# Two layers over neighbour lists on one core: one multiply per list in layer 0; gates ahead of a shared projection and slots added in pairs in layer 1

## The chip, the core and the metric

The kernel runs on one core of a Trainium2 chip. The metric is the device time of one execution in microseconds. The core's engines run side by side, each through its own instructions in order: PE (matrix multiplies; PEld is its weight load), DVE (vector), ACT (scalar), POOL (GpSimd) and SP (used here to issue DMAs). They wait for each other through semaphores. Data moves between the chip's memory (HBM) and the on-chip memories, SBUF (128 partitions) and PSUM (the accumulators of PE), by 16 DMA engines.

## The reference

There are 3327 nodes with 512 features and one sparse symmetric 0/1 adjacency matrix. Layer 0 is an attention layer with four heads of 128, layer 1 a gated sum of an attention part and a plain neighbour sum. Each layer is added to its input and normalised.

```python
# layer 0
feats = jnp.einsum('nf,hfo->hno', X, W)
e_s = jnp.einsum('hno,ho->hn', feats, a_self)
e_n = jnp.einsum('hno,ho->hn', feats, a_neigh)
logits = e_s[:, :, None] + e_n[:, None, :]
logits = jnp.where(logits > 0, logits, LRELU_ALPHA * logits)
logits = logits + NEG_INF * (1.0 - A)[None, :, :]
attn = jax.nn.softmax(logits, axis=-1)
out = jnp.einsum('hnm,hmo->hno', attn, feats)
...
x = _layernorm(x + relu(out + b))
# layer 1 (adj_a and adj_b are the same matrix)
attn_a = sigmoid(concatenate([adj @ x, x]) @ Wa.T + ba)
attn_b = sigmoid(concatenate([adj @ x, x]) @ Wb.T + bb)
h = x @ W_sa
scores = s_left[:, None] + s_right[None, :]
e = jnp.where(adj != 0, jnp.exp(-leaky_relu(scores, 0.01)), 0.0)
attn = e / (jnp.sum(e, axis=1, keepdims=True) + 1e-05)
x_a = attn @ h
x_b = adj @ (x @ W_gcnb) + b_gcnb
x = _layernorm(x + sigmoid(attn_a * x_a + attn_b * x_b))
```

## The kernel before

The kernel doesn't multiply with the adjacency matrix. A first stage reads it once, turns each node's row into a list of neighbour numbers, computes layer 0's features and attention logits for every node, and writes them as rows of 520 numbers into a table in HBM (`table0`). The nodes are sorted by the length of their lists and dealt into 26 tiles of 128, so that the tiles' lists have the fixed lengths in `CAPS`, from 23 slots down to 5, 253 in all. Tile 0 is handled as two lists of 12 and 11 slots, each other tile as one list: 27 lists.

Both layers then go tile by tile, in groups of four (`GRP`). `gather` (line 368) issues one indirect DMA per slot on POOL (line 373): 128 rows of the table, one per partition, into slot s of a buffer `g` of up to 15 slots. There are three such buffers in each layer, so the gather of a list waits until the list three before it has been read by all that use it.

Layer 0 (`attend`, line 403) fetches the tile's x rows (line 406), adds the logits (line 413), takes a softmax over the slots (lines 416 to 428, with the exponential on ACT), and multiplies each slot's 512 features by the attention of its head. That last step is one DVE instruction per slot (line 437), except for each third slot, where ACT does it in four instructions, one per head (line 435). PE sums the slots in PSUM by multiplying them with the identity (line 442); an fp32 matmul goes through PE in two passes. DVE adds bias and x, and takes the statistics. After each group the tiles are normalised (line 470) and `publish` (line 448) writes them as rows of a second table, `table1`, again by an indirect DMA on POOL (line 458). Layer 1's gathers read `table1`, so they start when the last tile has been published.

Layer 1 (`combine`, line 487) gathers a list in the same way, forms the attention weights `e` (lines 492 to 498) and their sum, and the two gates, `gate[:, 0:1]` and `gate[:, 1:2]`, from columns of the gathered rows (lines 503 to 511); `gate[:, 3:4]` is the first gate divided by the sum of e. PE sums all slots unweighted into `acc` (line 518, one PSUM bank). DVE sums them weighted by e into `sw`, one instruction per slot (lines 520 and 522). Both sums are transposed by PE (line 529), copied by ACT (lines 524 and 531), and multiplied by their own weight matrices into two banks, `pa` and `pb` (line 534). Lines 538 to 540 apply the gates to the two products and add them, on ACT and DVE. Then come the sigmoid (as a tanh, line 542), the residual, the statistics, and after each group of four the normalisation (line 552) and the write of the output rows, indirect DMAs on POOL (line 553).

The order of the instructions on each engine is not the order of the source: a scheduler places them by its own estimates. So a publish or an output write stands between gathers on POOL's queue, the logits of one list among another list's DVE work, and parts of one tile's `acc` ahead of the projections of the tile before it on PE. A dense version of the layers follows under a flag, for inputs whose lists don't fit; it does not run here.

Of the kernel before, what the change touches and what calls it, by code (L numbers as in the profile page):

```python
# [8 lines left out]
F32 = mybir.dt.float32  # L9
AF = mybir.ActivationFunctionType  # L10
ALU = mybir.AluOpType
# [3 lines left out]
P = 128  # L15
# [41 lines left out]
def sparse_pass(  # L57
# [28 lines left out]
    nc = tc.nc  # L86
    N, F = out.shape
    NP = x.shape[0]
    H, _, FO = W0.shape
    KT = F // P  # L90
# [11 lines left out]
    ident = const.tile([P, P], F32, name="ident")  # L102
# [5 lines left out]
    bias_g = const.tile([P, F], F32, name="bias_g")  # L108
# [10 lines left out]
    with tc.tile_pool(name="p0", bufs=1) as p0, tc.tile_pool(name="p0s", bufs=2) as p0s:  # L119
# [73 lines left out]
        with tc.tile_pool(name="p0f", bufs=2, space=PSUM) as psf, tc.tile_pool(  # L193
            name="p0c", bufs=1, space=PSUM
        ) as psc, tc.tile_pool(name="p0v", bufs=2, space=PSUM) as psv:
            for c0 in range(0, NP, CH):
# [7 lines left out]
                for g0 in range(0, NT, 4):  # L204
                    g = min(4, NT - g0)
                    a = p0s.tile([P, 4, CH], F32, tag="at", name=f"at{c0}_{g0}", bufs=10)
# [5 lines left out]
                for t in range(t0, t0 + nt):  # L212
                    pf = psf.tile([P, 2, 512], F32, tag="pf", name=f"pf{t}")
                    for k in range(KT):
                        for hh in range(2):
                            nc.tensor.matmul(  # L216
                                pf[:, hh, :HC], xc[:, k, (t - t0) * P : (t - t0 + 1) * P], w0[:, k, hh, :],
                                start=(k == 0), stop=(k == KT - 1),
# [8 lines left out]
                for half, m0, m1 in ((0, 0, 16), (1, 16, NT)):  # L227
                    for m in range(m0, m1):
                        s, c = (m - m0) // 4, (m - m0) % 4
                        nc.tensor.matmul(  # L230
                            pc[32 * c : 32 * c + 32, half, :cw], pow2[:, s, :], at[m // 4][:, m % 4, :cw],
                            start=(s == 0), stop=(m + 4 >= m1),
# [55 lines left out]
        with tc.tile_pool(name="p0r", bufs=1, space=PSUM) as psr:  # L288
# [46 lines left out]
            pb = psr.tile([P, 1], F32, name="pbad")  # L335
# [14 lines left out]
        with nc.allow_non_contiguous_dma(reason="four vectors of 512, onto partitions"):  # L350
            for i, w in enumerate((Wa, Wb)):
                for s in range(2):
                    src = w[0:1, s * F : (s + 1) * F].rearrange("o (k p) -> p (o k)", p=P)
# [48 lines left out]
    with tc.tile_pool(name="m0", bufs=2) as m0, tc.tile_pool(name="m0p", bufs=2, space=PSUM) as ps:  # L402
        def attend(j, mv):
            c = CAPS[j]
            xg = m0.tile([P, F], F32, tag="xg", name=f"xg{j}", bufs=3)
            nc.gpsimd.indirect_dma_start(
                out=xg, out_offset=None, in_=x, in_offset=bass.IndirectOffsetOnAxis(ap=own[:, j, :], axis=0)
            )
            got = gather(m0, table0, j, "g0")
            w = m0.tile([P, S, H], F32, tag="w", name=f"w{j}")  # L410
            lk = m0.tile([P, S, H], F32, tag="lk", name=f"lk{j}")
            for s0, n, g in got:
                nc.vector.tensor_add(  # L413
                    w[:, s0 : s0 + n, :], g[:, :n, F : F + H], es[:, j : j + 1, :].to_broadcast([P, n, H])
                )
            nc.vector.scalar_tensor_tensor(w[:, :c], w[:, :c], 0.2, w[:, :c], ALU.mult, ALU.max)
            mx = m0.tile([P, 1, H], F32, tag="mx", name=f"mx{j}")


            nc.vector.tensor_scalar(lk[:, :c, 0], valid[:, j, :c], 1e30, -1e30, ALU.mult, ALU.add)  # L420
            nc.vector.tensor_add(w[:, :c], w[:, :c], lk[:, :c, 0:1].to_broadcast([P, c, H]))
            nc.vector.tensor_reduce(mx[:, 0, :], w[:, :c].rearrange("p s h -> p h s"), AX.X, ALU.max)
            nc.vector.tensor_sub(w[:, :c], w[:, :c], mx.to_broadcast([P, c, H]))  # L423
            nc.scalar.activation(w[:, :c], w[:, :c], AF.Exp)  # L424
            den = m0.tile([P, 1, H], F32, tag="den", name=f"den{j}")
            nc.vector.tensor_reduce(den[:, 0, :], w[:, :c].rearrange("p s h -> p h s"), AX.X, ALU.add)
            nc.vector.reciprocal(den, den)
            nc.vector.tensor_mul(w[:, :c], w[:, :c], den.to_broadcast([P, c, H]))  # L428
            acc = ps.tile([P, F], F32, tag="acc", name=f"acc{j}")
            for s0, n, g in got:  # L430
                for s in range(s0, s0 + n):
                    gv = g[:, s - s0, 0:F].rearrange("p (h o) -> p h o", h=H)
                    if s % 3 == 2:
                        for h in range(H):
                            nc.scalar.activation(gv[:, h, :], gv[:, h, :], AF.Copy, scale=w[:, s, h : h + 1])  # L435
                    else:
                        nc.vector.tensor_tensor(  # L437
                            gv, gv,
                            w[:, s, :].rearrange("p (h o) -> p h o", o=1).to_broadcast([P, H, FO]),
                            ALU.mult,  # L440
                        )
                    nc.tensor.matmul(acc, ident, g[:, s - s0, 0:F], start=(s == 0), stop=(s == c - 1))  # L442
            y = x1[:, j, 0:F]
            nc.vector.tensor_add(y, acc, bias0)
            nc.vector.scalar_tensor_tensor(y, y, 0.0, xg, ALU.max, ALU.add)
            stats(m0, y, mv)

        def publish(j):
            pt = ps.tile([P, KT, P], F32, tag="pt", name=f"x1t{j}")
            for k in range(KT):  # L450
                nc.tensor.transpose(pt[:, k, :], x1[:, j, k * P : (k + 1) * P], ident)
            xt1 = m0.tile([P, KT, P], F32, tag="xt1", name=f"xt1_{j}")
            nc.scalar.copy(xt1, pt)
            pcol = ps.tile([P, NCOL], F32, tag="pcol", name=f"pcol{j}")
            for k in range(KT):
                nc.tensor.matmul(pcol, xt1[:, k, :], v1[:, k, :], start=(k == 0), stop=(k == KT - 1))
            nc.scalar.copy(x1[:, j, F : F + NCOL], pcol)
            nc.gpsimd.indirect_dma_start(
                out=table1[:, :], out_offset=bass.IndirectOffsetOnAxis(ap=own[:, j, :], axis=0),
                in_=x1[:, j, :], in_offset=None, bounds_check=N - 1, oob_is_err=False,  # L460
            )


        for js in groups:
            mv = m0.tile([P, GRP, 2], F32, tag="mv", name=f"mv0_{js[0]}")
            for i, j in enumerate(js):
                attend(j, mv[:, i, :])
            r = rsqrt(m0, mv, len(js), f"0_{js[0]}")
            for i, j in enumerate(js):
                nc.vector.tensor_scalar(  # L470
                    x1[:, j, 0:F], x1[:, j, 0:F], mv[:, i, 0:1], r[:, i : i + 1], ALU.subtract, ALU.mult
                )
                publish(j)


    with tc.tile_pool(name="w1", bufs=1) as w1, tc.tile_pool(name="m1", bufs=2) as m1, tc.tile_pool(
        name="m1p", bufs=2, space=PSUM
    ) as ps:
        wsa = w1.tile([P, KT, F], F32, name="wsa")
        nc.sync.dma_start(wsa, W_sa.rearrange("(k p) o -> p k o", p=P))  # L480
        wg = w1.tile([P, KT, F], F32, name="wg")
# [5 lines left out]
        def combine(j, mv):  # L487
            c = CAPS[j]
            got = gather(m1, table1, j, "g1")
            e = m1.tile([P, S], F32, tag="e", name=f"e{j}")  # L490
# [6 lines left out]
            gate = m1.tile([P, 6], F32, tag="gate", name=f"gate{j}")  # L497
# [12 lines left out]
            nc.scalar.activation(gate[:, 0:2], gate[:, 0:2], AF.Tanh, scale=0.5)  # L510
            nc.vector.tensor_scalar(gate[:, 0:2], gate[:, 0:2], 0.5, 0.5, ALU.mult, ALU.add)
            nc.vector.tensor_mul(gate[:, 3:4], gate[:, 0:1], gate[:, 2:3])

            acc = ps.tile([P, F], F32, tag="acc", name=f"acc1_{j}", bufs=1)
            sw = m1.tile([P, F], F32, tag="sw", name=f"sw{j}")
            for s0, n, g in got:
                for s in range(s0, s0 + n):
                    nc.tensor.matmul(acc, ident, g[:, s - s0, 0:F], start=(s == 0), stop=(s == c - 1))  # L518
                    if s == 0:
                        nc.vector.tensor_scalar(sw, g[:, 0, 0:F], e[:, 0:1], None, ALU.mult)  # L520
                    else:
                        nc.vector.scalar_tensor_tensor(sw, g[:, s - s0, 0:F], e[:, s : s + 1], sw, ALU.mult, ALU.add)  # L522
            sp = m1.tile([P, F], F32, tag="sp", name=f"sp{j}")
            nc.scalar.copy(sp, acc)  # L524
            outs = []
            for src, wt, tag in ((sw, wsa, "pa"), (sp, wg, "pb")):
                pt = ps.tile([P, KT, P], F32, tag="pt", name=f"pt{tag}{j}")
                for k in range(KT):
                    nc.tensor.transpose(pt[:, k, :], src[:, k * P : (k + 1) * P], ident)  # L529
                sT = m1.tile([P, KT, P], F32, tag="sT", name=f"sT{tag}{j}")  # L530
                nc.scalar.copy(sT, pt)
                po = ps.tile([P, F], F32, tag=tag, name=f"{tag}{j}")
                for k in range(KT):
                    nc.tensor.matmul(po, sT[:, k, :], wt[:, k, :], start=(k == 0), stop=(k == KT - 1))  # L534
                outs.append(po)
            za = m1.tile([P, F], F32, tag="za", name=f"za{j}", bufs=GRP + 2)
            zb = m1.tile([P, F], F32, tag="zb", name=f"zb{j}")
            nc.scalar.activation(za, outs[0], AF.Copy, scale=gate[:, 3:4])
            nc.vector.tensor_add(zb, outs[1], bias_g)
            nc.vector.scalar_tensor_tensor(za, zb, gate[:, 1:2], za, ALU.mult, ALU.add)  # L540

            nc.scalar.activation(za, za, AF.Tanh, scale=0.5)
            nc.vector.scalar_tensor_tensor(za, za, 0.5, x1[:, j, 0:F], ALU.mult, ALU.add)
# [446 lines left out]
```

## Time and profile before

| | us |
|---|---|
| median of 3 runs (lowest, highest) | 1273.58 (1273.38, 1276.06) |
| the profiled execution | 1273.58 |
| its span | 1271.8 |
| lists and table 0, to 206 | 206 |
| lists written to HBM and read back, 206 to 274 | 68 |
| layer 0: first x rows to the first gather of layer 1, 274 to 712 | 438 |
| layer 1: to the last output write, 712 to 1258 | 546 |

The span runs from the first to the last recorded instruction; the time of the execution has 1.8 us more around it. The stages overlap by little, because layer 0 needs all lists and layer 1 all published rows. The profile page gives for the whole span:

```profile
PE 906.7 (71%) x2790; PEld 456.8 (36%) x2790; DVE 693.0 (54%) x2045; ACT 219.4 (17%) x639; POOL 657.6 (52%) x688
```

These shares are means over stages of different kinds, and no engine is near 100%. What a change in a stage is worth must be read within that stage, from what the engines wait for there. A group's line in the profile reads: line of the source, engine, operation, what is written from what, count, then the busy time in us, the mean of one instruction in ns, and the idle time of the engine just ahead of such instructions with what ended most of it. A timeline's line reads: start and length in us, engine, line, operation, count if several equal ones follow each other, and in brackets the idle time before it and what ended it; "issue" is idle time in which the profile shows nothing waited for.

### The profile page before, as it was taken

To read this page: it belongs to the slowest core of one execution; us is meant where nothing else is said; L and a number is where in the kernel's file an instruction comes from. 1 tells how busy PE (TensorE), PEld (TensorE's weight loads), DVE (VectorE), ACT (ScalarE), POOL (GpSimd) and SP (SyncE) were. 2 spreads that over 40 slices of the span, in tenths; PEclk is the share of its full clock that TensorE was granted. 3 is DMA by queue.
4 is the path that set the end of the run, shared out by engine and by line. 5 is a ranking of instruction groups with operands and counts; after the bars stand their busy time and mean duration, and the time that the engine had idled before them with its cause. 6 is when DMAs were issued, how large, how long until landed. Compare 5 with 4: busy or idle time off the path is not lost. (4 is left out here: it accounts for less than half of the span.)

```text
span 1271.8 us, 10106 instructions
## 1 busy us (share of the span) xinstructions
PE 906.7 (71%) x2790; PEld 456.8 (36%) x2790; DVE 693.0 (54%) x2045; ACT 219.4 (17%) x639; POOL 657.6 (52%) x688
## 2 busy tenths in 40 slices
PE   3999941001985869798677475796996969989891
PEld 1756520000433325444234122343443434444440
DVE  4599893002555564557565046755565555756551
ACT  0101100001233222323132001111111111222220
POOL 4201102347777777777772577746546554554410
PEclk9999975555987987788797698898998999989996
DMA  9999920038777676766761687745446444344400
GB/s 312 394 394 392 380 74 3 7 81 213 210 211 200 181 202 199 211 186 195 206 198 63 200 200 202 198 123 148 129 119 174 119 136 131 113 132 117 133 26 27
DMA packets 87809, 220.72 MB, mean 174 GB/s; under 512 B 17056, under 2 KB 23360, under 8 KB 87744
## 3 DMA queue, kind: packets, MB, share of 16 engines
q0 software_dynamic: 49664, 162.66, 45.1%
q1 hardware_dynamic: 34288, 54.69, 12.0%
q10 hardware_dynamic: 3792, 2.63, 0.7%
q8 instruction: 25, 0.41, 0.1%
q14 instruction: 40, 0.33, 0.1%
HBM read 198.85 MB, written 21.09 MB: 173 GB/s over the span
## 5 line engine op out<-in xcount | busy, mean ns | idle before, releaser
L373 POOL DMA_INDIRECT g<-table,srt x506 | 520.5, 1029 | 243.0 <-issue 140.3
L442 PE MATMUL acc<-g,ident 128*128 128x512 f32 x506 | 259.8, 672 | 86.5 <-DVE g L437 76.1
L518 PE MATMUL acc<-g,ident 128*128 128x512 f32 x506 | 240.7, 616 | 27.5 <-DMA g<-table,srt 24.4
L442 PEld LDWEIGHTS acc<-g,ident 128*128 128x128 f32 x506 | 105.9, 216 | 223.4 <-issue 142.3
L522 DVE SCALAR_TENSOR_TENSOR sw<-g,e,sw 128x512 f32<-128x512 f32 x227 | 168.4, 750 | 6.1
L518 PEld LDWEIGHTS acc<-g,ident 128*128 128x128 f32 x506 | 94.9, 196 | 145.5 <-issue 110.0
L437 DVE TENSOR_TENSOR g<-g,w 128x512 f32<-128x512 f32 x178 | 114.9, 695 | 0.7
L216 PE MATMUL pf<-w,xc 128*128 128x260 f32 x416 | 99.0, 392 | 18.4 <-DVE w L183 18.4
L492 DVE TENSOR_SCALAR e<-g,x1s 128x10 f32<-128x10 f32 (+10 forms) x27 | 6.3, 234 | 185.6 <-DMA g<-table,srt 182.8
L534 PE MATMUL pa<-wsa,sTpa 128*128 128x512 f32 x208 | 100.6, 629 | 0.0
L435 ACT ACTIVATE g<-g,w 128x128 f32<-128x128 f32 x300 | 90.8, 388 | 22.9 <-DVE w L428 17.5
L534 PE MATMUL pb<-wg,sTpb 128*128 128x512 f32 x208 | 93.5, 592 | 0.0
L216 PEld LDWEIGHTS pf<-w,xc 128*128 128x128 f32 x416 | 78.7, 194 | 36.3 <-DVE w L183 20.1
L413 DVE TENSOR_TENSOR w<-g,srt 128x40 f32<-128x40 f32 (+10 forms) x27 | 5.4, 199 | 146.0 <-DMA g<-table,srt 116.0
L224 POOL DMA_DIRECT2D table<-row x26 | 14.2, 546 | 122.8 <-ACT st L223 112.9
L553 POOL DMA_INDIRECT out<-za,srt x26 | 28.0, 1078 | 88.0 <-DVE za L552 64.9
L534 PEld LDWEIGHTS pa<-wsa,sTpa 128*128 128x128 f32 x208 | 43.5, 209 | 57.7 <-issue 54.0
L424 ACT ACTIVATE w<-w 128x40 f32<-128x40 f32 (+11 forms) x26 | 6.1, 236 | 336.7 <-DVE w L423 154.8
L319 POOL DMA_INDIRECT lists<-st,ranki x26 | 25.3, 971 | 71.4 <-DMA lists<-st,ranki 36.3
L529 PE MATMUL ptpb<-ident,sp 128*128 128x128 f32 x104 | 20.2, 325 | 55.9 <-ACT sp L524 55.9
L534 PEld LDWEIGHTS pb<-wg,sTpb 128*128 128x128 f32 x208 | 39.5, 190 | 49.7 <-issue 49.7
L336 PE MATMUL pbad<-bad,ones 128*128 128x1 f32 x2 | 0.6, 362 | 76.6 <-DVE bad L334 76.6
(153 smaller groups left out, 898.9 us busy)
## 6 DMA issues: line engine op xcount, KB each, us to landing
at<-in_adjT SPq DMA_DIRECT2D x36, 1024.0 KB, 15.8
g<-table,srt POOLq DMA_INDIRECT x506, 3.7
table<-row POOLq DMA_DIRECT2D x26, 260.0 KB, 5.6
xc<-in_xT SPq DMA_DIRECT2D x6, 1024.0 KB, 14.7
at<-in_adjT SPq DMA_DIRECT2D x12, 512.0 KB, 13.6
w<-in_W SPq DMA_DIRECT2D x4, 256.0 KB, 7.6
wsa<-in_W_sa ACTq DMA_DIRECT2D x1, 1024.0 KB, 11.1
wsa<-in_W_sa SPq DMA_DIRECT2D x1, 1024.0 KB, 6.1
```

The lines of the kernel that those rows point to most:

```text
L216: nc.tensor.matmul(pf[:, hh, :HC], xc[:, k, (t - t0) * P : (t - t0 + 1) * P], w0[:, k, hh, :], start=(k == 0), stop=(k == KT - 1),)
L224: nc.gpsimd.dma_start(table0[t * P : (t + 1) * P, :], row)
L319: nc.gpsimd.indirect_dma_start(out=lists[:, :], out_offset=bass.IndirectOffsetOnAxis(ap=ranki[:, t : t + 1], axis=0), in_=st[:, t, :], in_ ...
L373: nc.gpsimd.indirect_dma_start(out=g[:, s - s0, :], out_offset=None, in_=table[:, :], in_offset=bass.IndirectOffsetOnAxis(ap=srt[:, j, s : ...
L435: nc.scalar.activation(gv[:, h, :], gv[:, h, :], AF.Copy, scale=w[:, s, h : h + 1])
L437: nc.vector.tensor_tensor(gv, gv, w[:, s, :].rearrange("p (h o) -> p h o", o=1).to_broadcast([P, H, FO]), ALU.mult,)
L442: nc.tensor.matmul(acc, ident, g[:, s - s0, 0:F], start=(s == 0), stop=(s == c - 1))
L518: nc.tensor.matmul(acc, ident, g[:, s - s0, 0:F], start=(s == 0), stop=(s == c - 1))
L522: nc.vector.scalar_tensor_tensor(sw, g[:, s - s0, 0:F], e[:, s : s + 1], sw, ALU.mult, ALU.add)
L529: nc.tensor.transpose(pt[:, k, :], src[:, k * P : (k + 1) * P], ident)
L534: nc.tensor.matmul(po, sT[:, k, :], wt[:, k, :], start=(k == 0), stop=(k == KT - 1))
L553: nc.gpsimd.indirect_dma_start(out=out, out_offset=bass.IndirectOffsetOnAxis(ap=own[:, j, :], axis=0), in_=z, in_offset=None, bounds_check ...
```

## The change

In layer 0 the multiplication by attention becomes one DVE instruction per list, over all its slots at once (up to 128 x 15 x 512 elements), in place of one per slot; ACT no longer takes part. The matmuls that sum the slots follow it.

In layer 1 four things change:

- The weights e are multiplied by the first gate and the reciprocal of their sum before they are used (one small DVE instruction per tile), and the unweighted sum is multiplied by the second gate when ACT copies it out of PSUM. With the gates already in them, both products are summed by PE in one bank, `po`, and one DVE instruction adds the gated bias. Lines 538 and 539 go.
- Of each list of n slots, floor(3n/8) pairs of slots are first added by DVE in place, and PE sums the pair as one slot. This is 83 pairs over all lists, so PE sums 170 slots instead of 253. The addition stands after the two instructions that need the slots unadded.
- `acc` has two banks instead of one.
- The two transposed sums have their own PSUM and SBUF buffers.

```diff
             for s0, n, g in got:
+                gv = g[:, :n, 0:F].rearrange("p s (h o) -> p s h o", h=H)
+                nc.vector.tensor_tensor(
+                    gv, gv,
+                    w[:, s0 : s0 + n, :].rearrange("p s (h o) -> p s h o", o=1).to_broadcast([P, n, H, FO]),
+                    ALU.mult,
+                )
                 for s in range(s0, s0 + n):
-                    gv = g[:, s - s0, 0:F].rearrange("p (h o) -> p h o", h=H)
-                    if s % 3 == 2:
-                        for h in range(H):
-                            nc.scalar.activation(gv[:, h, :], gv[:, h, :], AF.Copy, scale=w[:, s, h : h + 1])
-                    else:
-                        nc.vector.tensor_tensor(
-                            gv, gv,
-                            w[:, s, :].rearrange("p (h o) -> p h o", o=1).to_broadcast([P, H, FO]),
-                            ALU.mult,
-                        )
                     nc.tensor.matmul(acc, ident, g[:, s - s0, 0:F], start=(s == 0), stop=(s == c - 1))
...
-            acc = ps.tile([P, F], F32, tag="acc", name=f"acc1_{j}", bufs=1)
+            nc.vector.tensor_scalar(e[:, :c], e[:, :c], gate[:, 3:4], None, ALU.mult)
+            acc = ps.tile([P, F], F32, tag="acc", name=f"acc1_{j}", bufs=2)
             sw = m1.tile([P, F], F32, tag="sw", name=f"sw{j}")
             for s0, n, g in got:
+                pairs = (3 * n) // 8
                 for s in range(s0, s0 + n):
-                    nc.tensor.matmul(acc, ident, g[:, s - s0, 0:F], start=(s == 0), stop=(s == c - 1))
+                    i = s - s0
                     if s == 0:
                         nc.vector.tensor_scalar(sw, g[:, 0, 0:F], e[:, 0:1], None, ALU.mult)
                     else:
-                        nc.vector.scalar_tensor_tensor(sw, g[:, s - s0, 0:F], e[:, s : s + 1], sw, ALU.mult, ALU.add)
+                        nc.vector.scalar_tensor_tensor(sw, g[:, i, 0:F], e[:, s : s + 1], sw, ALU.mult, ALU.add)
+                    if i < 2 * pairs and i % 2 == 0:
+                        continue
+                    if i < 2 * pairs:
+                        nc.vector.tensor_add(g[:, i, 0:F], g[:, i - 1, 0:F], g[:, i, 0:F])
+                    nc.tensor.matmul(acc, ident, g[:, i, 0:F], start=(s == (1 if pairs else 0)), stop=(s == c - 1))
...
-            nc.scalar.copy(sp, acc)
...
+            nc.scalar.activation(sp, acc, AF.Copy, scale=gate[:, 1:2])
+            po = ps.tile([P, F], F32, tag="po", name=f"po{j}")
...
-                    nc.tensor.matmul(po, sT[:, k, :], wt[:, k, :], start=(k == 0), stop=(k == KT - 1))
+                    nc.tensor.matmul(po, sT[:, k, :], wt[:, k, :], start=(i + k == 0), stop=(i + k == KT))
...
-            nc.scalar.activation(za, outs[0], AF.Copy, scale=gate[:, 3:4])
-            nc.vector.tensor_add(zb, outs[1], bias_g)
-            nc.vector.scalar_tensor_tensor(za, zb, gate[:, 1:2], za, ALU.mult, ALU.add)
+            nc.vector.scalar_tensor_tensor(za, bias_g, gate[:, 1:2], po, ALU.mult, ALU.add)
```

More of the change, by code (lines that the diff above doesn't have):

```diff
@@ L521, in combine @@
                     else:
-                        nc.vector.scalar_tensor_tensor(sw, g[:, s - s0, 0:F], e[:, s : s + 1], sw, ALU.mult, ALU.add)
+                        nc.vector.scalar_tensor_tensor(sw, g[:, i, 0:F], e[:, s : s + 1], sw, ALU.mult, ALU.add)
[4 more added lines that the diff above has]
+                    nc.tensor.matmul(acc, ident, g[:, i, 0:F], start=(s == (1 if pairs else 0)), stop=(s == c - 1))
             sp = m1.tile([P, F], F32, tag="sp", name=f"sp{j}")
-            nc.scalar.copy(sp, acc)
-            outs = []
-            for src, wt, tag in ((sw, wsa, "pa"), (sp, wg, "pb")):
-                pt = ps.tile([P, KT, P], F32, tag="pt", name=f"pt{tag}{j}")
+            nc.scalar.activation(sp, acc, AF.Copy, scale=gate[:, 1:2])
+            po = ps.tile([P, F], F32, tag="po", name=f"po{j}")
+            for i, (src, wt, tag) in enumerate(((sw, wsa, "a"), (sp, wg, "b"))):
+                pt = ps.tile([P, KT, P], F32, tag=f"pt{tag}", name=f"pt{tag}{j}")
                 for k in range(KT):
                     nc.tensor.transpose(pt[:, k, :], src[:, k * P : (k + 1) * P], ident)
-                sT = m1.tile([P, KT, P], F32, tag="sT", name=f"sT{tag}{j}")
+                sT = m1.tile([P, KT, P], F32, tag=f"sT{tag}", name=f"sT{tag}{j}")
                 nc.scalar.copy(sT, pt)
-                po = ps.tile([P, F], F32, tag=tag, name=f"{tag}{j}")
                 for k in range(KT):
-                    nc.tensor.matmul(po, sT[:, k, :], wt[:, k, :], start=(k == 0), stop=(k == KT - 1))
-                outs.append(po)
+                    nc.tensor.matmul(po, sT[:, k, :], wt[:, k, :], start=(i + k == 0), stop=(i + k == KT))
             za = m1.tile([P, F], F32, tag="za", name=f"za{j}", bufs=GRP + 2)
-            zb = m1.tile([P, F], F32, tag="zb", name=f"zb{j}")
-            nc.scalar.activation(za, outs[0], AF.Copy, scale=gate[:, 3:4])
-            nc.vector.tensor_add(zb, outs[1], bias_g)
-            nc.vector.scalar_tensor_tensor(za, zb, gate[:, 1:2], za, ALU.mult, ALU.add)
+            nc.vector.scalar_tensor_tensor(za, bias_g, gate[:, 1:2], po, ALU.mult, ALU.add)
             nc.scalar.activation(za, za, AF.Tanh, scale=0.5)
```

## The prediction

> **What bounds the kernel now.** I read the stretches first, then the groups, then POOL's and DVE's timeline side by side. The chain of waits holds four pieces after 1252.8 us, the last output writes, and says nothing about the rest.
>
> The stretches: length, then busy time of PE, PEld, DVE, ACT and POOL, then clock, DMA share and GB/s. The first line is layer 0, the second layer 1.
>
> ```profile
> 274.00:712.00 438.00, 305.90 (x820) 155.35 (x820) 227.94 (x635) 115.28 (x378) 304.16 (x305) 0.80 0.67 191
> 712.00:1258.00 546.00, 450.23 (x1130) 203.80 (x1130) 306.10 (x756) 84.02 (x182) 296.82 (x279) 0.93 0.49 136
> ```
>
> Neither POOL nor PE looks full in layer 0, but POOL's timeline (start, length, idle before) shows a gather every 1.25 us without a pause: 0.95 busy and 0.30 to start the next.
>
> ```profile
> 439.36 0.94 POOL L373 DMA_INDIRECT g<-table,srt  x1 [0.30 <-issue]
> 440.61 1.39 POOL L373 DMA_INDIRECT g<-table,srt  x1 [0.30 <-issue]
> 442.31 0.95 POOL L373 DMA_INDIRECT g<-table,srt  x1 [0.30 <-issue]
> ```
>
> From 274.26 to 670.18 POOL starts 299 indirect DMAs: 395.9 us, of which 299 x 1.255 = 375 is this undisturbed pace. Layer 0 is bound by POOL's issue; PE, DVE and ACT wait for rows.
>
> The second line above is the important one. Its gather took 1.39, not 0.95. On DVE at that moment:
>
> ```profile
> 440.49 5.04 DVE L437 TENSOR_TENSOR g<-g,w 128x512 f32<-128x512 f32 x8
> ```
>
> Eight multiplies, one each 0.62 us. The gather began 0.12 after the first of them and was 0.44 late, so it went on 0.56 after that multiply's start, when it was nearly done. Gathers in the timeline that start 0.25, 0.33 and 0.05 after such a start (350.18, 384.29, 488.53) are 0.32, 0.23 and 0.50 late: a gather started inside a two-input DVE instruction stands still [...] then continues. The next gathers fall on the boundaries and lose nothing. Over layer 0 this costs 9.3 us. In layer 1 the same is seen with L522, whose pitch of 0.78 doesn't fit: each gather is 0.32 late.
>
> ```profile
> 752.33 1.27 POOL L373 DMA_INDIRECT g<-table,srt  x1 [0.30 <-issue]
> 753.90 1.27 POOL L373 DMA_INDIRECT g<-table,srt  x1 [0.30 <-DVE sw L522]
> ```
>
> The groups (busy, mean ns, idle before):
>
> ```profile
> L373 POOL DMA_INDIRECT g<-table,srt x506 | 520.5, 1029 | 243.0 <-issue 140.3
> L518 PE MATMUL acc<-g,ident 128*128 128x512 f32 x506 | 240.7, 616 | 27.5 <-DMA g<-table,srt 24.4
> L522 DVE SCALAR_TENSOR_TENSOR sw<-g,e,sw 128x512 f32<-128x512 f32 x227 | 168.4, 750 | 6.1
> L437 DVE TENSOR_TENSOR g<-g,w 128x512 f32<-128x512 f32 x178 | 114.9, 695 | 0.7
> L435 ACT ACTIVATE g<-g,w 128x128 f32<-128x128 f32 x300 | 90.8, 388 | 22.9 <-DVE w L428 17.5
> ```
>
> In layer 1 PE is 82% busy, and POOL waits for it to free a list's buffer:
>
> ```profile
> 990.77 0.95 POOL L373 DMA_INDIRECT g<-table,srt  x1 [10.02 <-PE acc L518]
> ...
> 1001.85 0.95 POOL L373 DMA_INDIRECT g<-table,srt  x1 [0.30 <-issue]
> 1007.56 1.35 POOL L373 DMA_INDIRECT g<-table,srt  x1 [4.76 <-PE acc L518]
> ```
>
> PE passes come at 0.43 us here (8 projection passes in 3.43), so a tile of nine slots is 18 x 0.43 + 16 x 0.43 + 1.3 of transposes + about 1 of gaps = 17 us, and acc ends at 990.3, 1007.1, 1023.2. Layer 1 is bound by PE, with stalls at each group of four.
>
> [...]
>
> **Layer 0, part by part.** Removed: 178 DVE multiplies of 0.63 pitch and 300 ACT ones. Both run beside POOL's issue, so their removal by itself is worth only the 9.3 us of small waits. Added: 27 multiplies, one per list of n = 5 to 15 slots. [...] 139.2 us in all, 8.2 for the longest. The build keeps each as a single instruction (128x15x512). Both inputs are in SBUF, and POOL always has a gather to issue.
>
> Behind the blocked gather stand all later gathers, the x rows and the publishes on the same queue. Per list: it is held from its own start, on average 0.63 (half of 1.25) after the multiply began, until about 0.13 before its end. So 139.2 - 27 x 0.13 - 27 x 0.63 = 118.7. The last list has no gathers behind it: -2. The old waits vanish: -9.3. Some of it falls on waits that POOL has anyway (a publish waits up to 3.0): -2. Lost: 105 us. Bounds [...]: 90 (the full 1.25 slips in each time, less is left) to 122. If a long instruction let POOL in between its rows: 0, the rival below. The first matmul of a list now waits for the whole multiply instead of one slot; that shows only in the last list, 2.8 against 0.7: +2. Buffers don't bind: with three lists and some 20 us of POOL time per list of ten, a list is free (3 landing + 2.5 logits + 5.5 + 10 on PE = 21) long before its turn at 40. Publishes stand one tile later in POOL's queue; that is not a new wait. Layer 0: +107.
>
> **Layer 1, part by part.** Removed from PE: floor(3n/8) slots per list, 83 in all, 2 passes of 0.43: 71 us if PE were the whole bound. The 16 projection passes per tile remain, merely into one bank; the second acc bank closes a gap of about 0.5 per tile. Removed from DVE: 26 additions at line 539 (0.69): -17.8; from ACT 26 scalings, which cost nothing where they are (the copy of acc becomes a scaled copy, one for one). Added on DVE: 83 additions at 0.63 (L437's pitch, same form): +52, and 26 small scalings of e: +4. DVE: 306 + 38 = 344 of some 510, not the bound.
>
> The new wait is PE's: a paired slot's matmul can start only after the two multiply-adds and the addition, and the pass order puts the first acc pass of tile j ahead of the projections of j-1. Also, DVE's order puts the logits of list j+1 ahead of the multiply-adds of list j, so these wait until that list has landed. That makes a loop. With S the start of tile j's multiply-adds and n = 9: first pair summed at S+2, acc 0.86, 16 projection passes 6.9, five more slots 4.3: buffer free at S+14.1. POOL then gathers list j+3, 9 x 1.42 = 12.8 (1.34 per gather in the stretch 990.8 to 1002.8 above, more for DVE's extra two-input work), 0.4 to start, 3.0 to land (1002.8 to the logits at 1005.8), 1.5 of small instructions, and S of tile j+2 follows: 31.8 for two tiles, 15.9 each. The same sum gives 18.9 for n = 12, 17.0 for 10, 14.7 for 8, 14 for 7, 12.9 and 12.2 for 6 and 5. From tile 5 to tile 25: 310, plus some 10 for the five group ends: 320, against 374 in the trace (839.4 to 1213.7). Gain 54. The last tile's end, with PE no longer a tile behind: 34 instead of 44, gain 10. Lost at the start: the first lists' acc now runs after the softmax, not on arrival, list 0 must be freed by DVE and PE before the gather of tile 2 goes on, and each of the next tiles waits for the list after it: walking the same loop from 749 puts tile 5 at 865 instead of 839: +26. Layer 1: -38. Bounds: -80 (PE's 71 and all stalls) to +10 (the loop 2.5 us longer per tile than I have it).
>
> **Sum.** The profiled execution took 1273.6 us (span 1271.8, 1.8 around it), which is the median of the runs. 1273.6 + 107 - 38 = 1342.6; I forecast 1342.
>
> **Rivals.** First: POOL isn't held by one long multiply, since the access pattern breaks it into rows. For it: the trace has no such long instruction. Against it: the waits end with instructions, and twice (474.40 and 590.99) lasted over two of them, 1.1 us. Then layer 0 is +2 and the time 1273.6 + 2 - 38 = 1238, faster. It decides from the hold per list: under 36/27 = 1.3 us each, the kernel gets faster. Chance 0.12.
>
> Second: POOL is held, and layer 1 gains nothing, because PE's wait for sums, the logits a list ahead and blocked gathers make the loop as long as PE's tile was: 1273.6 + 107 + 5 = 1386. For it: POOL's 10 us waits are already this loop. Against it: 14 to 17 us per tile by the rows above. Chance 0.15.
>
> That the long multiplies are not built as such is excluded by the order of the build.
>
> **How the numbers follow.** The likeliest case, 0.73, spans 1305 to 1375 by its bounds. Leaving out the first rival and the far half of the second gives the range, 1288 to 1390. A change within 0.2% (2.5 us) can't be told from none. Faster is the first rival, 0.12; exactly between it and the rest 0.02; slower 0.86.
>
> **What would show it.** In the changed profile: layer 0 some 540 us long instead of 438; 27 multiplies of 2.8 to 8.2 us; one gather of up to 8 us within each, the others still 0.95; ACT nearly idle there. In layer 1, 340 acc passes instead of 506, POOL's waits for acc still there, PE's waits now on DVE's sums, and 500 to 515 us in all. If gathers of 0.95 are seen inside a long multiply, the forecast is wrong and the first rival holds; if layer 1 is 540 or more, the second.

## The result, and the profile after

| | before | after |
|---|---|---|
| median, us (lowest to highest) | 1274.82 (1273.38 to 1279.97) | 1375.55 (1365.19 to 1380.27) |
| ratio, 95% interval | | 1.077 (1.070 to 1.084) |
| the profiled execution (its span) | 1273.58 (1271.8) | 1377.77 (1376.0) |
| lists written and read back | 68 | 70 |
| layer 0 | 438 | 556.3 |
| layer 1 | 546 | 529.7 |

The kernel became slower by 104 us in the profiled execution: 118 lost in layer 0, 16 gained in layer 1, 2 lost ahead of both. The forecast was 1342. Its signs were right in both layers; layer 0 lost 11 more than forecast and layer 1 gained 22 less. The result lies inside the forecast's range, 1288 to 1390, but just above the 1375 that its likeliest case allowed.

The two stretches of the layers after (length, busy time of PE, PEld, DVE, ACT, POOL, the share of PE's full clock that was granted, DMA share, GB/s):

```profile
276.00:832.30 556.30, 323.01 (x820) 162.00 (x820) 253.76 (x485) 24.66 (x78) 409.00 (x305) 0.75 0.53 150
832.30:1362.00 529.70, 396.10 (x964) 177.83 (x964) 339.20 (x839) 69.48 (x156) 291.78 (x279) 0.85 0.50 140
```

In layer 0 POOL is "busy" for 409 us instead of 304 with the same 305 instructions, and in layer 1 PE is busy 54 us less, but at a clock of 0.85 instead of 0.93. These two readings are followed here. The first, on POOL's timeline and on DVE's at the same moment:

```profile
343.46 0.94 POOL L373 DMA_INDIRECT g<-table,srt  x1 [0.30 <-issue]
344.70 7.84 POOL L373 DMA_INDIRECT g<-table,srt  x1 [0.30 <-issue]
352.85 1.03 POOL L373 DMA_INDIRECT g<-table,srt  x1 [0.30 <-issue]
```

```profile
343.57 8.16 DVE L432 TENSOR_TENSOR g<-g,w 128x7680 f32<-128x7680 f32 x1
```

The gather that started 1.13 us into the multiply ended as if it had been held until 0.14 us before the multiply's end and had then taken its usual 0.95. The gather of 343.46, begun 0.11 before the multiply, was not touched. The groups (busy, mean ns, idle before):

```profile
L373 POOL DMA_INDIRECT g<-table,srt x506 | 601.4, 1189 | 240.0 <-issue 146.0 <-PE acc L526 79.8 <-PE acc L438 6.3
L526 PE MATMUL acc<-g,ident 128*128 128x512 f32 x340 | 172.6, 645 | 104.6 <-DVE g L525 103.9
L432 DVE TENSOR_TENSOR g<-g,w 128x5120 f32<-128x5120 f32 (+10 forms) x27 | 139.2, 5160 | 0.7
L537 PE MATMUL po<-wsa,sTa 128*128 128x512 f32 x208 | 112.7, 693 | 0.0
```

The 27 multiplies take 139.2 us, as forecast, the longest 8.16. The trace of before gives nearly the same as an estimate: DVE takes 0.695 us over 512 elements (L437) and 1.218 over 1024 (L176), so 0.523 for each further slot and 0.172 once per instruction, and 253 x 0.523 + 27 x 0.172 = 137. The acc passes of layer 1 are two for each of the 170 slots, as the 506 were for 253. An acc pass now waits for DVE's sum (103.9 us in all), and POOL's waits for acc in layer 1 are as long as before (79.8, was 79.5). The last line matters below: a projection pass takes 693 ns as the profile counts, although most of them come at 430.

The second reading, on PE's timeline around tile 11:

```profile
1087.18 1.12 PE L526 MATMUL acc<-g,ident 128*128 128x512 f32 x2
1088.14 3.60 PE L537 MATMUL po<-wsa,sTa 128*128 128x512 f32 x8
1091.57 3.60 PE L537 MATMUL po<-wg,sTb 128*128 128x512 f32 x8
1095.01 5.31 PE L526 MATMUL acc<-g,ident 128*128 128x512 f32 x12
1100.16 0.60 PE L533 MATMUL pta<-ident,sw 128*128 128x128 f32 x4
1106.83 2.08 PE L526 MATMUL acc<-g,ident 128*128 128x512 f32 x2 [6.07 <-DVE g L525]
1108.69 5.38 PE L537 MATMUL po<-wsa,sTa 128*128 128x512 f32 x8
```

Tile 10's passes come without a pause; tile 11's first pair is waited for during 6.07 us, and the ten passes behind that pause take 2.08 + 5.38 us where the same ten took 1.12 + 3.60. The granted clock fell at that moment (columns as for the stretches above, the clock third from the end):

```profile
1085.00:1105.00 20.00, 15.30 (x44) 7.03 (x42) 12.63 (x30) 3.73 (x8) 14.47 (x15) 1.00 0.60 174
1106.80:1112.00 5.20, 5.17 (x6) 2.19 (x7) 5.03 (x8) 0.00 (x0) 3.98 (x5) 0.50 0.72 198
```

This returns in every second tile. ACT's timeline shows why nothing else fills the pause:

```profile
1102.94 0.20 ACT L506 ACTIVATE gate<-gate 128x2 f32<-128x2 f32 x1 [6.32 <-DVE gate L505]
1103.05 0.20 ACT L492 ACTIVATE e<-e 128x9 f32<-128x9 f32 x1
1103.15 0.67 ACT L528 ACTIVATE sp<-acc,gate 128x512 f32<-128x512 f32 x1
```

The scaling of tile 10's acc, which PE had finished by 1100.3, stands in ACT's queue behind a gate of tile 11 and the exponential of tile 12, and DVE's queue has held both back for tile 12's list, which landed at 1102.5.

### The profile page after: what moved, and what is told of

The parts are those of the page before. It is cut to its first block, busy times and chain, and to the rows that moved or that the text cites. A ratio compares the mean times of both kernels' runs of the same rounds, so it can differ in the third digit from the quotient of the medians.

```text
span 1376.0 us, 9195 instructions
## 1 busy us (share of the span) xinstructions
PE 870.1 (63%) x2624; PEld 437.7 (32%) x2624; DVE 751.4 (55%) x1977; ACT 114.2 (8%) x313; POOL 757.4 (55%) x688
## 5 line engine op out<-in xcount | busy, mean ns | idle before, releaser
L373 POOL DMA_INDIRECT g<-table,srt x506 | 601.4, 1189 | 240.0 <-issue 146.0
L438 PE MATMUL acc<-g,ident 128*128 128x512 f32 x506 | 275.1, 704 | 190.7 <-DVE g L432 190.7
L526 PE MATMUL acc<-g,ident 128*128 128x512 f32 x340 | 172.6, 645 | 104.6 <-DVE g L525 103.9
L438 PEld LDWEIGHTS acc<-g,ident 128*128 128x128 f32 x506 | 111.6, 228 | 337.8 <-issue 170.0
L432 DVE TENSOR_TENSOR g<-g,w 128x5120 f32<-128x5120 f32 (+10 forms) x27 | 139.2, 5160 | 0.7
L526 PEld LDWEIGHTS acc<-g,ident 128*128 128x128 f32 x340 | 65.3, 202 | 184.6 <-issue 119.7
L537 PE MATMUL po<-wsa,sTa 128*128 128x512 f32 x208 | 112.7, 693 | 0.0
L537 PE MATMUL po<-wg,sTb 128*128 128x512 f32 x208 | 96.5, 607 | 4.9 <-ACT sTb L535 4.9
L537 PEld LDWEIGHTS po<-wsa,sTa 128*128 128x128 f32 x208 | 47.1, 230 | 62.7 <-issue 60.3
L454 POOL DMA_INDIRECT table<-x1s,srt x26 | 34.5, 1328 | 52.6 <-ACT x1s L453 19.1
L525 DVE TENSOR_TENSOR g<-g 128x512 f32<-128x512 f32 x83 | 57.4, 691 | 2.1
L537 PEld LDWEIGHTS po<-wg,sTb 128*128 128x128 f32 x208 | 39.8, 194 | 57.6 <-issue 47.1
```

The source lines that it names most:

```text
L373: nc.gpsimd.indirect_dma_start(out=g[:, s - s0, :], out_offset=None, in_=table[:, :], in_offset=bass.IndirectOffsetOnAxis(ap=srt[:, j, s : ...
L432: nc.vector.tensor_tensor(gv, gv, w[:, s0 : s0 + n, :].rearrange("p s (h o) -> p s h o", o=1).to_broadcast([P, n, H, FO]), ALU.mult,)
L454: nc.gpsimd.indirect_dma_start(out=table1[:, :], out_offset=bass.IndirectOffsetOnAxis(ap=own[:, j, :], axis=0), in_=x1[:, j, :], in_offset ...
L525: nc.vector.tensor_add(g[:, i, 0:F], g[:, i - 1, 0:F], g[:, i, 0:F])
L526: nc.tensor.matmul(acc, ident, g[:, i, 0:F], start=(s == (1 if pairs else 0)), stop=(s == c - 1))
L537: nc.tensor.matmul(po, sT[:, k, :], wt[:, k, :], start=(i + k == 0), stop=(i + k == KT))
```

## The experiments

Unless said otherwise a kernel was timed in three rounds beside the kernel before on the same chip. One thing has to be known to read the times: in three of the four groups the kernel before took 1338 to 1343 us, not 1275. By the profiles of kernels that share a layer with it, most of the difference lies in its layer 0, 490 instead of 438 us, and some ten more in its layer 1, 554 to 558 us instead of 544 to 548; this is the subject of the sixth experiment. So times are compared within a group, as ratios, and mechanisms by the stages of the profile.

**1. Each half alone.** The first kernel has only the new multiply of layer 0, the second only the new layer 1; the other layer is that of before.

> Only the layer 0 half of the change: one multiply per list, layer 1 as before. If a gather stands still for the whole of a long two-input multiply, layer 0 grows by what the profile after shows, 115 to 118 us, and the time is 1390 (1380 to 1397); the prediction's own sum of 107 would give 1382. If the loss in layer 0 were only the way that both layers meet, or came from something else than the multiply, it would lie below 1340; if POOL is not held, at 1276.

> Only the layer 1 half: gates ahead, one shared projection, pairs; layer 0 as before. By the profile after, layer 1 is 16 us shorter than before: 1258 (1253 to 1263). If layer 1 was hurt by starting after a changed layer 0, the prediction's 38 us come back: 1237. If layer 1 gains nothing of its own: 1275.

Measured: ratio 1.043 (1.038 to 1.049), 1403 us, and 0.979 (0.974 to 0.984), 1318 us. The absolute times missed, here and in experiments 2 and 3, because the kernel before stood at 1343 in this group. The stages held: layer 0 with the multiply takes 552.0 us, and 118.8 of its POOL time lies above 0.95 us per indirect DMA (119.2 in the profile after, 14.4 in the one before: POOL's busy time in layer 0 less 305 x 0.95); the new layer 1 takes 530.2, as after. Neither loss nor gain comes from the meeting of the halves. That the ratio of the first is only 1.043 follows from the 490 us beside it: 552 - 490 = 62. The second gains 25 us and not 16, because the old layer 1 is slower on this chip too: 557.9 us in the first kernel's profile.

**2. The same multiplies in pieces.**

```diff
+                for q in range(0, n, 4):
+                    m = min(4, n - q)
+                    gv = g[:, q : q + m, 0:F].rearrange("p s (h o) -> p s h o", h=H)
+                    nc.vector.tensor_tensor(
+                        gv, gv,
+                        w[:, s0 + q : s0 + q + m, :].rearrange("p s (h o) -> p s h o", o=1).to_broadcast([P, m, H, FO]),
+                        ALU.mult,
+                    )
```

> Layer 0 alone, the multiply of a list cut into instructions of 4 slots (2.29 us each instead of up to 8.2), same work on DVE, ACT as idle as after; layer 1 as before. If the hold belongs to the single instruction, one gather (1.25 us with its issue) gets through at each boundary: walking gathers of 0.95 + 0.30 past these lengths over random starts loses 68 us, less the 12 us of small waits of before: layer 0 +56 (45 to 68), time 1331 (1320 to 1343). If the loss comes from DVE's busy time in two-input work, or from ACT's share having moved to DVE, or from matmuls waiting, the time stays near that of the uncut multiply, 1380 to 1390.

The other size is one slot per instruction, still all on DVE (timed once, in the group where the kernel before took 1277):

> Layer 0 alone, all 253 multiplies on DVE as one instruction per slot, none on ACT: DVE has the same elements to multiply as after, in pieces of 0.69 us. If the hold belongs to the single instruction, walking gathers past these pieces loses 7 us, as many as before within a few: long gathers together 7 to 18 us over layer 0, ratio 0.99 to 1.01. If DVE's load or ACT's lost share is what costs, 60 us and more.

| slots per multiply | POOL's time above 0.95 per indirect DMA in layer 0 | expected | layer 0 | layer 0 of before on such a chip |
|---|---|---|---|---|
| whole list (5 to 15) | 118.8 | 115 to 118 | 552.0 | 490 |
| 4 | 73.1 | 68 | 508.5 | 490 |
| 1 | 23.1 | 7 to 18 | 452.0 | 442.8 |

The loss follows the length of the instruction, at the same number of multiplied elements and with ACT nearly idle in all three (24 to 25 us). POOL's timeline of the pieces of four shows a gather getting through at each boundary (compare 7.84 us for one held gather above):

```profile
461.54 2.31 POOL L373 DMA_INDIRECT g<-table,srt  x1 [0.30 <-issue]
464.15 1.90 POOL L373 DMA_INDIRECT g<-table,srt  x1 [0.30 <-issue]
466.36 1.36 POOL L373 DMA_INDIRECT g<-table,srt  x1 [0.31 <-DMA g<-table,srt]
```

On DVE three multiplies, of 4, 4 and 3 slots, run from 460.74 to 466.90; three gathers are held, 1.36, 0.95 and 0.41 us. The 2.29 us of a piece of four agrees with the profile after, where five slots take 2.82 and each further one 0.53 more. The ratio of the pieces of four is 1.008 (1.005 to 1.012); the single pieces took 1292 against 1277: 1.012, a little above the expected ratio, and without an interval. Their 23.1 us of held gathers, too, are more than the 7 to 18 expected, and 8.7 more than before: the walk past the pieces priced them too low.

**3. The same multiply with one input in PSUM.**

```diff
-            nc.vector.tensor_mul(w[:, :c], w[:, :c], den.to_broadcast([P, c, H]))
+            wp = ps.tile([P, S, H], F32, tag="wp", name=f"wp{j}")
+            nc.vector.tensor_mul(wp[:, :c], w[:, :c], den.to_broadcast([P, c, H]))
...
-                    w[:, s0 : s0 + n, :].rearrange("p s (h o) -> p s h o", o=1).to_broadcast([P, n, H, FO]),
+                    wp[:, s0 : s0 + n, :].rearrange("p s (h o) -> p s h o", o=1).to_broadcast([P, n, H, FO]),
```

> Layer 0 alone, one multiply per list as after, but the weights are written to a PSUM tile, so that the multiply has one input in SBUF and one in PSUM; layer 1 as before. If two SBUF inputs are what holds the gather, no gather is longer than 0.95 in these multiplies, the small waits of before vanish too, and the time is 1265 (1258 to 1280). If any long DVE instruction holds POOL, whatever its inputs, 1390.

DVE's timeline has the same long instruction, and POOL's timeline at that moment runs through it undisturbed:

```profile
331.89 8.15 DVE L433 TENSOR_TENSOR g<-g,wp 128x7680 f32<-128x7680 f32 x1
```

```profile
333.48 0.94 POOL L373 DMA_INDIRECT g<-table,srt  x1 [7.30 <-PE acc L439]
334.73 0.94 POOL L373 DMA_INDIRECT g<-table,srt  x1 [0.30 <-issue]
335.98 0.95 POOL L373 DMA_INDIRECT g<-table,srt  x1 [0.30 <-issue]
337.23 0.94 POOL L373 DMA_INDIRECT g<-table,srt  x1 [0.30 <-issue]
338.48 0.95 POOL L373 DMA_INDIRECT g<-table,srt  x1 [0.30 <-issue]
```

Over layer 0 POOL's time above 0.95 is 2.5 us instead of 118.8. So it is not the length as such: with both inputs in SBUF a multiply of 8.16 us held the gather, with one of them in PSUM a multiply of 8.15 us did not. The time did not follow as expected: ratio 1.005 (1.003 to 1.007), layer 0 507 us against 490. POOL now waits longer: 86 us in all up to the last gather, 48 of them put down to acc, as in the first line above, and 20 to what the profile calls remote. The layer 0 of before has 60 us of such waits on such a chip (experiment 6), so 26 came with this kernel. What it takes on a chip with the 438 us layer 0 was not measured.

**4. What makes layer 1's gain.** One kernel without the pairs, one with a fourth gather buffer, one with extra work in PE's pause; all have the layer 0 of before.

```diff
-                pairs = (3 * n) // 8
+                pairs = 0
```

> Layer 0 of before, layer 1 of after without the pairs: every slot goes through TensorE again (506 acc passes instead of 340), gates ahead and one shared projection bank as after. If the pairs carry the gain, layer 1 is as before or longer, 540 to 555. If the folding and the second acc bank carry it, and the pairs only trade PE's passes for waits, 520 to 535, the same as with pairs.

Layer 1 takes 542.8 us, against 528.7 with pairs on the same chip (the first kernel of experiment 5). So the pairs are worth 14 us, of the 71 that they take from PE. What the folding and the second acc bank are worth isn't settled: the old layer 1 took 554 to 558 us in the profiles from chips of this kind and 544 to 548 in the others. Ratio 0.991 (0.987 to 0.995).

```diff
-            got = gather(m1, table1, j, "g1")
+            got = gather(m1, table1, j, "g1", 12, 4)
```

The two added numbers are the slots per buffer and the buffers.

> Layer 0 of before, layer 1 of after, but layer 1 gathers into four buffers of 12 slots instead of three of 15 (lists of 13 to 23 slots split in two). If the loop of the prediction (multiply-adds, buffer free, gather, landing, multiply-adds two tiles on) bounds layer 1, a fourth buffer opens it, POOL's waits for acc (80 us) mostly go, PE's 6 us pauses in every second tile too, and with them the slow passes after them: layer 1 480 us (465 to 500) instead of 530. If the order of the engines' queues bounds it (logits of the next list ahead, projections behind the first pair), or TensorE's clock by itself, layer 1 stays at 520 to 535.

```profile
769.40:1258.00 488.60, 378.60 (x966) 170.60 (x966) 342.63 (x847) 70.35 (x156) 294.75 (x279) 0.89 0.54 152
```

Layer 1 is 488.6 us long, inside the expected band, and POOL's waits for acc fall, as the group lines of the kernel with three buffers (the second of experiment 1) and of this one show:

```profile
L373 POOL DMA_INDIRECT g<-table,srt x506 | 517.0, 1022 | 268.4 <-issue 161.3 <-PE acc L530 77.6 <-PE acc L442 16.5
L373 POOL DMA_INDIRECT g<-table,srt x506 | 514.9, 1018 | 224.6 <-issue 166.5 <-PE acc L530 28.1 <-remote 12.1
```

The smaller buffers also split the lists of tiles 1 to 3. That isn't where the gain lies: up to tile 5 this layer 1 takes 17 us longer than with three buffers, and from tile 5 to tile 25, where no list is split, 284.8 us instead of 344.0. Counted without their names, POOL's waits ahead of layer 1's gathers fall from 77 to 39 us. DVE and POOL have about the same work as with three buffers (343 against 339 us and 295 against 295), and PE as many passes, so the 42 us were neither DVE's load nor the number of PE's passes: the loop through the buffer bounded the layer, as the prediction had it. Part of the gain comes by way of the clock, which rose from 0.86 to 0.89: PE is busy 379 us with these passes instead of 391. Ratio 0.959 (0.951 to 0.967).

```diff
-                pt = ps.tile([P, KT, P], F32, tag=f"pt{tag}", name=f"pt{tag}{j}")
+                pt = ps.tile([P, KT, P], F32, tag=f"pt{tag}", name=f"pt{tag}{j}", bufs=2 - i)
...
+                if i == 0 and j % 2 == 0 and j >= 6:
+                    warm = ps.tile([P, F], F32, tag="warm", name=f"warm{j}", bufs=1)
+                    for _ in range(6):
+                        nc.tensor.matmul(warm, ident, sw, start=True, stop=True)
```

> Layer 0 of before, layer 1 of after, with six extra matmuls (5.2 us, into a bank that nothing reads, computing nothing that is used) after the first four transposes of each even tile from 6 on, where PE pauses for 6 us. If it is the pause that makes the eight projection passes behind it take 5.4 us instead of 3.6, these passes go back to 3.4 to 3.6 and layer 1 gets shorter, 529.7 to about 510 (500 to 522), although PE has more to do. If PE's work itself bounds layer 1, its added 52 us show: 540 or more. If neither, 525 to 535.

Layer 1 took 567.1 us, ratio 1.002 (0.998 to 1.006). That is in the band named for PE's work as the bound, but the time is no clean test, because the edit did more than fill a pause: the bank for the extra work was taken from `ptb` (the first changed line), and PE then paused elsewhere, as its timeline shows:

```profile
1045.20 5.32 PE L541 MATMUL warm<-sw,ident 128*128 128x512 f32 x12
1051.65 3.70 PE L545 MATMUL po<-wsa,sTa 128*128 128x512 f32 x8 [1.13 <-ACT sp L532]
1055.19 0.60 PE L537 MATMUL ptb<-ident,sp 128*128 128x128 f32 x4
1055.62 1.02 PE L530 MATMUL acc<-g,ident 128*128 128x512 f32 x2
1062.87 2.93 PE L545 MATMUL po<-wg,sTb 128*128 128x512 f32 x3 [6.22 <-ACT sTb L543]
```

Behind the filled pause the eight passes take 3.70; behind the new one, the first three alone take 2.93. The same is seen over the layer: the 208 wsa passes, 80 of them behind filled pauses, take 101.9 us instead of the 108.3 in the second kernel of experiment 1, and the 208 wg passes 108.2 instead of 96.7. The slow passes went with the pause. Whether filling every pause would shorten the layer was not shown.

**5. The better version.** The PSUM weights with layer 1 of after, with three buffers and with four:

> One multiply per list with its weights in PSUM, and layer 1 of after. The hold in layer 0 is gone (long gathers together under 5 us over layer 0, against 119), layer 1 is 530. On a chip where layer 0 of before takes 438: 428 + 530, time 1248, ratio 0.98 (0.97 to 0.99). On a chip where engines stand without a visible cause in layer 0 of before (490), as in the runs so far: 507 + 530, time 1325, ratio 0.987 (0.975 to 1.0). If any long instruction holds POOL, ratio 1.03 or more.

Ratio 0.989 (0.981 to 0.997); layer 0 494.6, layer 1 528.7, POOL's time above 0.95 in layer 0 3.5.

> Layer 0 with one multiply per list and its weights in PSUM, layer 1 of after with four gather buffers: the candidate for the best. Where layer 0 of before takes 490: layer 0 495, layer 1 488, time 1286, ratio 0.959, the same as with the layer 0 of before. Where it takes 438: layer 0 428 to 440, time 1210, ratio 0.95 (0.94 to 0.965).

Ratio 0.963 (0.956 to 0.970), layer 0 504, layer 1 487. The layer 0 of before with four buffers (0.959, in another group) can't be told apart from it and needs no PSUM bank for the weights. These two are the best kernels of this study, faster than the kernel before and than the changed one. On a chip with the 438 us layer 0 neither was run. The multiply with its weights in PSUM, free of the hold, has not made layer 0 shorter in any of its three runs: 494 to 507 us, against 490 to 494 for the layer 0 of before on such chips.

**6. The changed kernel and the kernel before once more.**

> The changed kernel once more, in one group with the next. In the last groups the kernel before took 1341 to 1343 instead of 1275, all of it in layer 0 (490 us instead of 438), where POOL waits 60 us for things other than the multiplies. If these waits and the hold overlap, since a POOL that stands still for the hold would have stood for them anyway, the changed kernel takes the same 1375 (1368 to 1385) there as with the fast layer 0, and the ratio is 1.026. If they add, it takes 1440, ratio 1.075 again. On a chip with the 438 us layer 0: 1375, ratio 1.077.

Measured: 1379.06 against 1337.85, ratio 1.031 (1.024 to 1.039), with layer 0 at 556.2 and layer 1 at 529.9. The changed kernel takes the same time on both kinds of chip, and the loss is 41 us on one and 101 on the other. Of the 60 us between the two losses some 52 are the layer 0 of before and some ten its layer 1.

> The kernel before, for a profile from the groups of these runs. Layer 0 should be 490 us with some 60 us of waits on POOL (7 us in the profile of before), and layer 1 555; the sum is the 1341 of its times. If layer 0 is 438 here, the 490 came with the edits to layer 1.

This group fell on a chip of the first kind: 1277.86, layer 0 442.8, layer 1 544.0. So the profile of the slow layer 0 is that of the kernel with only the new layer 1, whose layer 0 is unchanged: 490.3 us, 60 of them POOL's waits for other things than the multiplies (7 in before). The order of the instructions is the same, and lists that DVE waits for land as quickly as before (median 3.0 us from the last gather to the logits in both). In one list ACT stands between multiplies most of which have nothing to wait for, where before starts one each 0.29 us:

```profile
323.15 0.40 ACT L435 ACTIVATE g<-g,w 128x128 f32<-128x128 f32 x1 [1.03 <-issue]
324.58 0.40 ACT L435 ACTIVATE g<-g,w 128x128 f32<-128x128 f32 x1 [1.03 <-issue]
325.98 0.40 ACT L435 ACTIVATE g<-g,w 128x128 f32<-128x128 f32 x1 [1.00 <-issue]
```

There are five pauses ahead of instructions without any wait in that layer 0, 4.8 us together, so they alone don't make the 52. For the rest the profile can't be asked: all those from the slower groups lack a large part of the semaphore records (`g<-table` has a median of 3.7 us from issue to landing in before, and none there), so that "issue" and "remote" in them often stand for a wait whose end was not recorded, and the names of other waits are less sure too. Whether the chip is the cause or something else that differed between the groups is open, since each group ran on one chip; no run here tells it. What is shown is that the slow layer 0 and the hold don't add: POOL's other waits in the changed kernel are 19 us here and 17 on the first kind of chip, and not 60. That the hold covers them is the likeliest reading, since with the same few instructions but no hold (experiment 3) they are back, 86 us; the profiles don't show it directly.

## Why the prediction came out as it did

**The hold in layer 0: right, size included.** The term was 139.2 - 27 x 0.13 - 27 x 0.63, less 2 for the last list: 116.7. In the profile after, 26 of POOL's indirect DMAs are held, one for each multiply but the last, together 114.8 us. The waits end 0.05 to 0.15 us before the multiply's end, so the 0.13 taken from instructions of 0.69 us holds for 8.16. The first rival decided at 1.3 us per list and the hold is 4.4: it fell, and the dose in experiment 2 and the PSUM input in experiment 3 show the cause. The hold was seen one way only: gathers that had begun before a multiply ran on, 0.94 to 0.99 us long, and the 27 multiplies beside them took no longer than the forecast 139.2.

**The other waits in layer 0: wrong sign.** "Some of it falls on waits that POOL has anyway (a publish waits up to 3.0): -2." POOL's waits for buffers and publishes became longer instead, from 7.2 to 17.1 us in all, above all for DVE's softmax results and for acc. The step counted what the hold might cover, and not that everything behind a list, acc and publish, now starts only when the whole list is multiplied. The small waits left as forecast (9.8 against 9.3), and the end of the layer cost 2.8 against 2. Sum: 114.8 - 9.8 + 9.9 + 2.8 = 117.7, against the 117.6 that the first gathers of the two layers show; forecast 107.

**The tile loop of layer 1: right mechanism, wrong size.** The start cost 26.8 us (forecast 26), the end gained 12 (forecast 10). The middle, from the multiply-adds of tile 5 (986.5) to those of tile 25 (1330.3), took 343.8, forecast 320, before 374.3: a gain of 30 where 54 was forecast. The term that failed is "16 projection passes 6.9": 0.43 per pass was read from a stretch in which PE did not pause. In the changed one PE pauses in every second tile, for the loop's own reason, and runs slower after it. Layer 1 after has 52 groups of eight projection passes. Forty take 3.60 to 3.70 us, at a granted clock of 1.00. The other twelve take 4.5 to 6.0 at a mean clock of 0.80 to 0.61, so that length times clock is 3.6 to 3.7 in each, and all twelve begin within 5.0 us of the end of a pause of 2.8 to 7.7 us. From tile 5 to 25 the time of the passes above 0.43 adds up to 22.8 us (15.6 in projections, 7.2 in acc), close to the 23.8 that are missing; that all of it lies on the loop is argued from the size. The slower passes go with the granted clock, 0.50 from 1106.8 to 1112.0, behind the pause, against 1.00 between 1085 and 1105; and the eight passes behind a filled pause took 3.70 again (experiment 4), though the time did not follow there. Why the clock falls behind a pause, no run here shows. The profile before held the warning: the first passes behind a pause of 11.7 us begin at 888.6, and eight passes from 891.2 on take 5.16, at a granted clock of 0.69.

The loop itself, from buffer to buffer, was shown by the fourth buffer. The second rival, layer 1 at 540 or more, fell at 529.7, but the 500 to 515 that the forecast gave as its own sign were missed too.

**The stage ahead** is 2.6 us longer (the first x rows are fetched at 276.86 instead of 274.26), which no step had. With 10.6 in layer 0 and 22 in layer 1 this makes the 35 us between 1342.6 and 1377.8: three misses of one direction, none of which hid another.

## What to carry to other kernels

In these runs one long DVE instruction over two SBUF inputs stopped a POOL queue of indirect DMAs from the first gather that began within it to 0.05 to 0.15 us before its end (7.84 us instead of 0.95 for a gather within a multiply of 8.16). Where POOL's issue is the bound, keep such instructions short (with pieces of one slot, 0.69 us, gathers were held 9 us more here than in the kernel before, with whole lists 104), or put the smaller input in PSUM, which took the hold away (2.5 us over layer 0 instead of 118.8) but, on the chips where it ran, did not make the layer shorter. Taking work off a bound engine doesn't bring its busy time when a buffer loop stands behind it; price the loop, and price the passes after each pause by what the trace shows there (eight took 4.5 to 6.0 us at a granted clock of 0.80 to 0.61, against 3.60 to 3.70 at 1.00), since the rate read from the busy PE did not hold for the one that waits. And a loss measured on one chip (101 us here) can be less than half of that on another (41) where the kernel compared with has waits of its own.

## What was not expected of the hardware

- A held gather is held until 0.14 us before the end of an 8.16 us instruction without a break (7.84 instead of 0.95 us), although its access pattern has 60 rows of 128 per partition.
- With one input in PSUM the same instruction takes the same time (8.15 against 8.16 us).
- The same kernel takes 1275 us on some chips and 1338 to 1343 on others, at an equal median from a list's last gather to its use (3.0 us); the profiles give no cause for the extra 52 us of layer 0.
